# Scan items in pairs, a fixed order for one thread, and attention's products with V one pair of heads later, in a two-layer mixer and expert kernel

## The chip, the cores and the metric
The kernel runs on one core of a Trainium2 chip, as one launch. The metric is the device time of a run in microseconds; lower is better. The core's engines each work through their own queue in order: PE (matmul), DVE (vector), ACT (activation functions), POOL (GpSimd), and SP, which issues most of the DMAs.

## What is computed
Eight rows (batch entries) of 512 tokens with 256 channels pass through two layers. Layer 0: a conditioning block (gates, nine exponential moving averages over time, a layer norm), a Mamba block (a state space scan with 16 states for each of 512 inner channels), a linear map chosen by row, and a mixture of experts (top 2 of 8). Layer 1: a feed-forward block with LoRA experts, attention with 8 heads, an adapter with a layer norm, and a mixture of experts (top 4 of 32) beside a shared expert. The parts that the change touches:

```python
# Mamba, for every time step
dA = jnp.exp(dlt[:, None, :] * A[None])
h = dA * h + dlt[:, None, :] * B_t[:, :, None] * x_t[:, None, :]
y_t = jnp.einsum('bn,bnd->bd', C_t, h) + D * x_t
# attention of layer 1
attn = jax.nn.softmax(jnp.einsum('bnhr,bmhr->bhnm', Q, K), axis=-1)
out = jnp.einsum('bhnm,bmhd->bnd', attn, V)
# adapter of layer 1
return (y - mu) * jax.lax.rsqrt(var + EPS) * g + b
```

## The kernel before
Channels lie on partitions, the 512 time steps of a row on columns; nearly all data is float32. Two Python generators write the program, and a planner (the framework's list scheduler) places each instruction on its engine by its simulated time, with the order of writing as the priority. The order on each engine is then fixed, and the framework adds the semaphores.

**Thread x** (`thread_x`, L367) does the conditioning and Mamba blocks. `head_a` (L442) and `head_b` (L519) compute one row's inputs of the scan. Each head product goes through one of two PSUM buffers `gx`, and the ACT or DVE instruction that reads it is written right behind it. `split3` (L328) splits a float32 tile into three bfloat16 parts. The softplus part (L551 to L576) writes (delta, delta*x) tiles `dd` and stores them to DRAM as `pack`. From there `get_pack` (L591) reads them back, replicated over four groups of 32 partitions: 32 channels by 4 states fill the 128 partitions.

`scan(b)` (L612) has 64 items for a row: 4 channel blocks j, 4 state groups g, 4 quarters k. For item i, `begin` (L619) writes the decay `dA` = Exp on ACT (L623) and the input `h` = packed * B on POOL (L625); `run` (L645) has the recurrence on DVE (L651, one scan instruction over 512 columns, in place in `h`) and the product with C, which lies in PSUM (L652); `add` (L654) sums over states with four PE matmuls against `fold`, each into another 32 partitions of the same PSUM tile `yp` (L660). `begin` runs two items ahead; `dA` has 4 buffers and `h` has 8. After four groups, y is gated (L664, L665), and after 64 items the output projection and the store to `xa` follow (L684, L686). Two steps of the next row's head are written with every two items, and what is left of them before item 58.

**Thread y** (`thread_y`, L711) takes groups of rows (GROUPS: row 0; 1 and 2; 3 to 5; 6 and 7) through the rest of layer 0 and layer 1's feed-forward and attention, ending in `xb`. For each row, LoRA weights are merged first (L827 to L845), then come four pairs of heads (L862). For a pair: projections of Q and K (L870), four steps of `scores` (L883), `values` (L876) and `turn` (L901), and 32 matmuls of the products with V (L923). In `scores`, PE makes two score tiles (L889; 64 partitions each, at two places of the array), DVE takes the negative row maximum (L893), ACT takes Exp with the row sum (L896), and DVE takes the reciprocal (L897) and multiplies (L898). `turn` transposes on PE (L906). Tiles there have one buffer each unless a number says otherwise.

While thread y is written for group q, thread x is written for group q+1, in proportion (constants XROW and others at L36). With the last group the routers of the last mixture (`top4`, L930) are written; they use `layernorm` (L87: Sqrt on ACT at L99, reciprocal on DVE at L100). Last come the experts (`expert_tile`, L1060) and the final gather.

Of the kernel before, what the change touches and what calls it, by code (L numbers as in the profile page):

```python
# [35 lines left out]
XROW, YROW, YGROUP, YTILE, P4ROW = 269.0, 242.0, 20.0, 9.0, 10.0  # L36
# [15 lines left out]
def adaln_attn_ffn_kernel(ctx: ExitStack, tc: tile.TileContext, d: dict, out: bass.AP):  # L52
# [34 lines left out]
    def layernorm(pool, ps_tile, o, bufs=1):  # L87

        mean = ps_tile()
        mm(mean, [(onesdiv, o[:, k, :]) for k in range(KC)])  # L90
        cen = pool.tile([P, KC, T], F32, tag="ln_c", name="ln_c", bufs=bufs)
        nc.vector.tensor_tensor(cen, o, rep(mean, KC), ALU.subtract)
        yield 1
        sq = pool.tile([P, KC, T], F32, tag="ln_q", name="ln_q", bufs=bufs)
        nc.gpsimd.tensor_tensor(sq, cen, cen, ALU.mult)  # L95
        var = ps_tile()
        mm(var, [(onesdiv, sq[:, k, :]) for k in range(KC)])
        rstd = pool.tile([P, T], F32, tag="ln_r", name="ln_r", bufs=bufs)
        nc.scalar.activation(rstd, var, AF.Sqrt, bias=epst)  # L99
        nc.vector.reciprocal(rstd, rstd)  # L100
        return cen, rstd
# [53 lines left out]

    members = {}
# [12 lines left out]
    SYNC = mybir.DependencyInfo(mybir.DependencyClass.Sync, mybir.DependencyReason.DATA)  # L169

# [157 lines left out]
    def split3(pool, src, outs, p0, p1):  # L328
# [3 lines left out]
        nc.scalar.copy(outs[0], src)  # L332
        nc.vector.tensor_tensor(r, src, outs[0], ALU.subtract)
        nc.scalar.copy(m, r)
        nc.gpsimd.tensor_tensor(r, r, m, ALU.subtract)
        nc.scalar.copy(outs[1], m)
# [30 lines left out]
    def thread_x(wp, wk, ps):  # L367
# [74 lines left out]
        def head_a(b):  # L442

            x = rows[b]
            pt = gx()
            mm(pt[:64, :], [(Wn1[:, k, :], x[:, k, :]) for k in range(KC)])
            h1 = wk.tile([64, T], F32, tag="sg", name="h1", bufs=2)
            nc.scalar.activation(h1, pt[:64, :], AF.Gelu, bias=col("bn1", p=64))
            yield 3
            pt = gx()  # L450
            mm(pt[:8, :], [(Wn2, h1)])
            m8 = wk.tile([8, T], F32, tag="tr", name="m8", bufs=2)
            nc.scalar.activation(m8, pt[:8, :], AF.Sigmoid, bias=col("bn2c", p=8))
            split3(wk, m8, [m3[0:8, :], m3[32:40, :], m3[64:72, :]], 0, 8)
            yield 4
            ct = wk.tile([P, KC, T], F32, tag="ct", name="ct")
            for k in range(KC):
                nc.vector.tensor_tensor_scan(
                    ct[:, k, :], alpha[:, 0:1].to_broadcast([P, T]), x[:, k, :], 0.0, ALU.mult, ALU.add)
                yield 1.3  # L460
            gated = wk.tile([P, KC, T], F32, tag="gated", name="gated")
            for e in range(KC):
                pt = gx()
                mm(pt, [(Wg[:, k, ts(e, P)], x[:, k, :]) for k in range(KC)]
                   + [(Wg[:, KC + k, ts(e, P)], ct[:, k, :]) for k in range(KC)])
                sg = wk.tile([P, T], F32, tag="sg", name="sg", bufs=2)
                nc.scalar.activation(sg, pt, AF.Sigmoid, bias=col("bg", e))
                nc.gpsimd.tensor_tensor(gated[:, e, :], x[:, e, :], sg, ALU.mult)
            yield 4
            temporal = wk.tile([P, KC, T], F32, tag="ct", name="temporal")  # L470
            for i in range(8):
                pt = gx()
                mm(pt, [(three[0:72, i : i + 1].to_broadcast([72, P]), m3)])
                gm = wk.tile([P, KC, T], F32, tag="gm", name="gm")
                nc.vector.scalar_tensor_tensor(gm, rep(pt, KC), 0.5, gated, ALU.add, ALU.mult)
                yield 1.5
                for k in range(KC):
# [8 lines left out]
                    yield 2.2  # L486
            soma = wk.tile([P, KC, T], F32, tag="gm", name="soma")
            for e in range(KC):
                pt = gx()
                mm(pt, [(Wsoma[:, k, ts(e, P)], x[:, k, :]) for k in range(KC)])  # L490
                nc.scalar.activation(soma[:, e, :], pt, AF.Gelu, bias=col("bsoma", e))
            yield 3
            for e in range(KC):
                pt = gx()
                mm(pt, [(Wtemp[:, k, ts(e, P)], temporal[:, k, :]) for k in range(KC)])
                sg = wk.tile([P, T], F32, tag="sg", name="sg", bufs=2)
                nc.scalar.activation(sg, pt, AF.Sigmoid, bias=col("btemp", e))
                nc.gpsimd.tensor_tensor(soma[:, e, :], soma[:, e, :], sg, ALU.mult)
            yield 3
            cen = wk.tile([P, KC, T], F32, tag="cen", name="cen")  # L500
            sq = wk.tile([P, KC, T], F32, tag="gated", name="sq")
            for e in range(KC):
                pt = gx()
                mm(pt, [(Wout[:, k, ts(e, P)], soma[:, k, :]) for k in range(KC)])
                nc.scalar.copy(cen[:, e, :], pt)
                nc.scalar.activation(sq[:, e, :], pt, AF.Square)
                yield 2
            pt = gx()
            mm(pt, [(onesdiv, sq[:, k, :]) for k in range(KC)])
            rstd = wk.tile([P, T], F32, tag="sg", name="rstd", bufs=2)  # L510
            nc.scalar.activation(rstd, pt, AF.Ln, bias=epst)
            nc.scalar.activation(rstd, rstd, AF.Exp, scale=-0.5)
            nc.vector.tensor_tensor(cen, cen, rep(rstd, KC), ALU.mult)
            yield 3
            rows[b] = cen
            if b + 1 < NB:
                get_row(b + 1)

        def head_b(b):  # L519

            cn = rows[b]
            xc = wk.tile([P, 4, T], F32, tag="xc", name="xc")
            for j in range(4):
                pt = gx()
                mm(pt, [(W_in[:, k, ts(j, P)], cn[:, k, :]) for k in range(KC)])
                xp = xps[j % 2]
                nc.scalar.activation(xp[:, 3:], pt, AF.Identity, bias=wb[:, j : j + 1])
                cv = xc[:, j, :]
                nc.scalar.activation(cv, pt, AF.Identity, scale=col("convw", 4 * j + 3), bias=cb[:, j : j + 1])
                for i in range(3):  # L530
                    nc.vector.scalar_tensor_tensor(
                        cv, xp[:, i : i + T], col("convw", 4 * j + i), cv, ALU.mult, ALU.add)
                yield 3
            nc.scalar.activation(xc, xc, AF.Silu)
            nc.sync.dma_start(xzs[b % 2][:, :, 0, :], xc)
            for j in range(4):
                pt = gx()
                mm(pt, [(W_in[:, k, ts(4 + j, P)], cn[:, k, :]) for k in range(KC)])
# [3 lines left out]
            yield 5  # L542
            pt = gx()
            mm(pt[:96, :], [(W_x[:, j, :], xc[:, j, :]) for j in range(4)])
            dt = wk.tile([64, T], F32, tag="dt", name="dt")
            nc.scalar.copy(dt, pt[:64, :])
            bc3 = wk.tile([96, T], BF16, tag="bc3", name="bc3", bufs=2)
            split3(wk, pt[64:96, :], [bc3[64:96, :], bc3[32:64, :], bc3[0:32, :]], 64, 96)
            yield 3

            for j2 in range(2):  # L551
                dds, es = [], []
                for j in (2 * j2, 2 * j2 + 1):
                    pt = gx()
                    mm(pt, [(W_dt[:, ts(j, P)], dt)])

                    dd = wk.tile([P, 2, T], F32, tag=("gated", "ct")[j % 2], name="dd")
                    e = wk.tile([P, T], F32, tag="sg", name="sp_e", bufs=2)
                    nc.scalar.activation(e, pt, AF.Abs, bias=col("bdt", j))
                    nc.vector.tensor_scalar(dd[:, 0, :], pt, col("bdt", j), 0.0, ALU.add, ALU.max)  # L560
                    nc.scalar.activation(e, e, AF.Exp, scale=-1.0)
                    u = dd[:, 1, :]
                    nc.vector.tensor_scalar(u, e, 1.0, None, ALU.add)
                    nc.vector.scalar_tensor_tensor(e, u, 1.0, e, ALU.subtract, ALU.subtract)
                    dds.append(dd)
                    es.append(e)
                yield 3
                for dd in dds:
                    nc.scalar.activation(dd[:, 1, :], dd[:, 1, :], AF.Ln)
                for j, dd, e in zip((2 * j2, 2 * j2 + 1), dds, es):  # L570
                    u = dd[:, 1, :]
                    nc.gpsimd.tensor_tensor(u, u, e, ALU.subtract)
                    nc.gpsimd.tensor_tensor(dd[:, 0, :], dd[:, 0, :], u, ALU.add)
                    nc.gpsimd.tensor_tensor(dd[:, 1, :], dd[:, 0, :], xc[:, j, :], ALU.mult)
                    nc.sync.dma_start(packs[b % 2][j], dd)
                yield 3  # L576
            rows[b] = bc3

# [33 lines left out]
        def scan(b):  # L612

            bc3 = rows[b]
            items = [(j, g, k) for j in range(4) for g in range(4) for k in range(4)]
            yps, Cs, hs, dAs, xz = {}, {}, {}, {}, {}
            y8 = wk.tile([P, 4, T], F32, tag="y8", name="y8")

            def begin(i):  # L619
                j, g, k = items[i]  # L620
                t = got[b, j, k]
                dA = wk.tile([P, T], F32, tag="dA", name="dA", bufs=4)
# [14 lines left out]
                if j == 3 and b + 1 < NB and g == 3:  # L637
# [4 lines left out]
                    if k == 3:  # L642
                        get_B4(b + 1, 0)
# [558 lines left out]
```

## Time and profile before

| what | us |
|---|---|
| median of 3 runs (lowest, highest) | 4274.81 (4264.85, 4278.79) |
| the profiled execution, its own time | 4252.41 |
| span of the profile, first to last instruction | 4250.6 |
| DVE busy | 2670.9 |
| PE busy | 3440.5 |
| ACT busy | 1672.2 |
| POOL busy | 1565.8 |
| mean granted PE clock (share of full) | 0.889 |

The span has stages. To 150 us there is the head of row 0 alone. Its scan runs to 395 us, with nothing else but row 1's head. Three stages follow in which both threads run. From 2940 us on, thread y runs with the routers; from 3784 us the experts; from 4181 us the final gather. The profiled execution is 22.4 us below the median of the runs. In a line of the profile, L651 is a line of the kernel's source; "mean ns" is the mean length of one instruction; "idle before" is how long the engine had stood still, with what ended that wait.

### The profile page before, as it was taken

Reading aid. Unit: us, or ns where it says so; the run is one execution under the profiler, and the core shown is the slowest. Engines: PE = TensorE matmul, PEld = TensorE weight load, DVE = VectorE, ACT = ScalarE, POOL = GpSimd, SP = SyncE. Lnnn points to the kernel's source line nnn. Section 1 sums busy time; section 2 is a strip of 40 time slices with the busy share of each in tenths; the row PEclk is TensorE's granted clock in tenths of the full one; section 3 lists DMA queues with packets and bytes.
Section 4 is the critical chain, followed back from the end, with each engine's and each line's share of the span. In section 5 each row is a group of like instructions: output and inputs, shape, how many; then the busy total and the mean of one; then the engine's idle time right before and its main releaser. Section 6 shows DMA issues by size and latency. Waiting matters only on the chain. (4 is left out here: it accounts for less than half of the span.)

```text
span 4250.6 us, 36891 instructions
## 1 busy us (share of the span) xinstructions
PE 3440.5 (81%) x10964; PEld 1694.3 (40%) x10964; DVE 2670.9 (63%) x4290; ACT 1672.2 (39%) x2741; POOL 1565.8 (37%) x1222
## 2 busy tenths in 40 slices
PE   4556686887687888888758899889988999978994
PEld 2111352332254233333327443333456444436773
DVE  4698957886966686796892547575432454443336
ACT  2535463455366346445433443242223233322222
POOL 0456535434635333433542323231043111134552
PEclk7677798988798898999879999899989999989996
DMA  3235455324456423333346312213043312117776
GB/s 105 101 108 180 187 162 170 106 98 156 177 176 209 135 102 118 134 122 109 139 165 234 122 63 77 68 36 104 15 163 136 93 41 70 36 50 245 248 237 224
DMA packets 159372, 554.78 MB, mean 131 GB/s; under 512 B 27730, under 2 KB 34289, under 8 KB 146756
## 3 DMA queue, kind: packets, MB, share of 16 engines
q1 hardware_dynamic: 135076, 501.35, 35.2%
q0 software_dynamic: 24096, 51.08, 3.3%
q8 instruction: 87, 1.43, 0.1%
q14 instruction: 113, 0.93, 0.1%
HBM read 453.00 MB, written 234.82 MB: 162 GB/s over the span
## 5 line engine op out<-in xcount | busy, mean ns | idle before, releaser
L625 POOL TENSOR_TENSOR h<-packed,B 128x512 f32<-128x512 f32 x512 | 792.5, 1570 | 1054.2 <-PE yp L660 746.7
L651 DVE TENSOR_TENSOR_SCAN h<-dA,h 128x512 f32<-128x512 f32 x512 | 791.0, 1571 | 126.3 <-ACT dA L623 67.2
L623 ACT ACTIVATE dA<-packed,Aexp 128x512 f32<-128x512 f32 x512 | 359.8, 720 | 656.4 <-DVE h L651 446.5
L160 POOL DMA_INDIRECT tok<-ys,to_i x310 | 311.9, 1006 | 497.9 <-DVE ys L808 237.7
L660 PE MATMUL yp<-h,fold 128*32 128x512 f32 x1024 | 349.7, 704 | 156.9 <-DVE h L652 140.6
L923 PE MATMUL acc<-aT,V 128*128 128x512 f32 x1024 | 453.4, 597 | 5.3 <-ACT aT L907 3.2
L160 POOL DMA_INDIRECT tab<-row,si x192 | 197.4, 1028 | 465.5 <-issue 210.5
L652 DVE TENSOR_TENSOR h<-h,c 128x512 f32<-128x512 f32 x512 | 330.5, 672 | 29.0 <-PE c L78 28.2
L923 PEld LDWEIGHTS acc<-aT,V 128*128 128x128 f32 x1024 | 193.2, 191 | 245.9 <-issue 235.1
L78 PE MATMUL acc<-wv,c 128*128 128x512 f32 x512 | 270.2, 642 | 0.4
L78 PE MATMUL g<-qk 64*128 64x512 f32 x512 | 210.7, 681 | 54.9 <-ACT ex L896 28.6
L896 ACT ACTIVATE ex<-g,nm 128x512 f32<-128x512 f32 x256 | 173.8, 684 | 157.5 <-DVE nm L893 157.3
L78 PE MATMUL g<-xT,fw 128*128 128x256 f32 x960 | 233.6, 396 | 2.5 <-ACT h L801 1.9
L893 DVE TENSOR_REDUCE nm<-g 128x1 f32<-128x512 f32 x256 | 165.0, 681 | 100.8 <-PE g L78 100.8
L78 PE MATMUL acc<-fw,h 128*128 128x256 f32 x960 | 221.6, 383 | 3.5 <-DVE ys L808 1.8
L78 PEld LDWEIGHTS g<-xT,fw 128*128 128x128 f32 x960 | 188.0, 201 | 39.4 <-issue 6.8
L78 PEld LDWEIGHTS acc<-fw,h 128*128 128x128 f32 x960 | 182.7, 192 | 41.6 <-issue 12.4
L906 PE MATMUL acc<-ident,ex 128*128 128x128 f32 x1024 | 160.3, 286 | 47.9 <-DVE ex L898 16.2
L906 PEld LDWEIGHTS acc<-ident,ex 128*128 128x128 f32 x1024 | 122.6, 146 | 188.4 <-issue 69.3
L660 PEld LDWEIGHTS yp<-h,fold 128*32 128x32 f32 x1024 | 44.7, 115 | 364.1 <-DVE h L652 208.3
L479 DVE TENSOR_TENSOR_SCAN tr<-alpha,gm 128x512 f32<-128x512 f32 x128 | 181.4, 1435 | 5.0 <-POOL y L665 3.5
L78 PE MATMUL g<-xT,mw 128*128 128x256 f32 x760 | 183.1, 385 | 0.0
(280 smaller groups left out, 5458.3 us busy)
## 6 DMA issues: line engine op xcount, KB each, us to landing
fw<-in_fW SPq DMA_DIRECT2D x60, 1154.0 KB
tab<-zeros SPq DMA_DIRECT2D x32, 2112.0 KB
packed<-pack SPq DMA_DIRECT2D x128, 512.0 KB
mw<-in_mW SPq DMA_DIRECT2D x95, 384.0 KB
tab<-zeros SPq DMA_DIRECT2D x16, 2080.0 KB
xt<-tab SPq DMA_DIRECT2D x95, 264.0 KB
xz<-xzs SPq DMA_DIRECT2D x32, 512.0 KB
pack<-dd SPq DMA_DIRECT2D x32, 512.0 KB
```

The lines of the kernel that those rows point to most:

```text
L78: nc.tensor.matmul(o, lhsT, rhs, start=(i == 0), stop=(i == len(pairs) - 1))
L160: i = nc.gpsimd.indirect_dma_start(out=table_, out_offset=bass.IndirectOffsetOnAxis(ap=idx, axis=0), in_=src, in_offset=None, bounds_check ...
L479: nc.vector.tensor_tensor_scan(tr, alpha[:, 1 + i : 2 + i].to_broadcast([P, T]), gm[:, k, :], 0.0, ALU.mult, ALU.add)
L623: nc.scalar.activation(dA, t[:, 0, :], AF.Exp, scale=A[:, 4 * j + k, g : g + 1])
L625: nc.gpsimd.tensor_tensor(h, t[:, 1, :], B4s[b, g], ALU.mult)
L651: nc.vector.tensor_tensor_scan(h, dAs.pop(i), h, 0.0, ALU.mult, ALU.add)
L652: nc.vector.tensor_tensor(h, h, Cs[0], ALU.mult)
L660: nc.tensor.matmul(yps[j][32 * k : 32 * k + 32, :], fold, hs.pop(i + k), start=(g == 0), stop=(g == 3))
L893: nc.vector.tensor_reduce(nm, sp, AX.X, ALU.max, negate=True)
L896: nc.scalar.activation(ex, sp, AF.Exp, bias=nm, accum_out=den)
L906: nc.tensor.transpose(tp[:, m, :], ex[:, ts(m, P)], ident)
L923: nc.tensor.matmul(ys[k], V[:, m, C * u + P * k : C * u + P * (k + 1)], aTs[u][:, m, :], start=(u == 0 and m == 0), stop=(u == 1 and m == 3))
```

## The change
- **Scan in pairs.** Items 2m and 2m+1 share one `h` tile of 2 x 512 columns (4 buffers) and one of two lasting decay tiles. Column 0 of the second half of a decay tile is set to zero once, so the second recurrence starts anew, and one scan instruction covers 1024 columns; the product with C likewise. One loop runs over the items of all 8 rows. Work that follows an item (fold, gate, output projection) is put in a list `due` some items later.
- **Head in finer steps.** `head_a` and `head_b` become one generator `head`, which yields between a product and the instruction that reads it; one step goes with each item, and a second one in every twelve items. The scan of a row may start when the first two channel blocks' packs are on their way.
- **Fixed order.** `in_order` ties each instruction of thread x to the one before it on the same engine, without a semaphore, so the planner can't reorder thread x within an engine. `chain` ties matmuls that go to different parts of the array (fold, score pairs, LoRA pairs) one behind the other.
- **Attention.** The steps are written out over pairs of heads, with the products with V of the pair before between the first scores of a pair. The softmax's division goes to ACT. The LoRA weights use the buffers of `V`, `aT`, `wv` and `qk`.
- **Layer norm.** Sqrt and reciprocal become Ln and Exp on ACT.

The diff, cut to its core (the head is shown by one of its parts):

```diff
-XROW, YROW, YGROUP, YTILE, P4ROW = 269.0, 242.0, 20.0, 9.0, 10.0
+XROW, YROW, YGROUP, YTILE, P4ROW = 256.0, 242.0, 20.0, 9.0, 10.0
...
-        nc.scalar.activation(rstd, var, AF.Sqrt, bias=epst)
-        nc.vector.reciprocal(rstd, rstd)
+        nc.scalar.activation(rstd, var, AF.Ln, bias=epst)
+        nc.scalar.activation(rstd, rstd, AF.Exp, scale=-0.5)
...
+    def in_order(X):
+        last = {}
+        while True:
+            n = len(nc.cur_bb.bb.instructions)
+            c = next(X, None)
+            for i in nc.cur_bb.bb.instructions[n:]:
+                if i.engine in last:
+                    tc.add_manual_dep(i, last[i.engine].name, NOSYNC)
+                last[i.engine] = i
...
+            def taps(pt, j):
+                nc.scalar.activation(xps[j % 2][:, 3:], pt, AF.Identity, bias=wb[:, j : j + 1])
...
+            pj = [project(W_in, cen, 0)]
+            yield
+            for j in range(4):
+                if j > 0:
+                    conv(j - 1)
+                taps(pj[j], j)
+                pj.append(project(W_in, cen, j + 1))
+                yield
...
+        decays = []
+        for i in range(2):
+            t = wp.tile([P, 2, T], F32, tag=f"dA{i}", name=f"dA{i}")
+            nc.vector.memset(t[:, 1, 0:1], 0.0)
+            decays.append(t)
+        def begin(n):
+            b, j, g, k = items[n]
+            t = got[b, j, k]
+            u = n % 2
+            nc.scalar.activation(decays[n // 2 % 2][:, u, u:], t[:, 0, u:], AF.Exp, scale=A[:, 4 * j + k, g : g + 1])
+            if u == 0:
+                hs[n // 2] = wk.tile([P, 2, T], F32, tag="h", name="h", bufs=4)
+            nc.gpsimd.tensor_tensor(hs[n // 2][:, u, :], t[:, 1, :], B4s[b, g], ALU.mult)
...
+        def scan(m):
...
+            nc.vector.tensor_tensor_scan(h, dA, h, 0.0, ALU.mult, ALU.add)
+        def read(m):
+            b, j, g, k = items[2 * m]
+            nc.vector.tensor_tensor(hs[m], hs[m], rep(Cs[0], 2), ALU.mult)
+            if k == 2:
+                due.setdefault(2 * m + 2, []).append(lambda: add(2 * m - 2))
...
+            chain([nc.tensor.matmul(
+                yps[0][32 * k : 32 * k + 32, :], fold, hh[k // 2][:, k % 2, :], start=(g == 0), stop=(g == 3))
+                for k in range(4)])
...
+        for n in range(N):
...
+            if n % 2 == 0:
+                scan(n // 2)
+            else:
+                read(n // 2)
+            if n + 2 < N:
+                begin(n + 2)
+            for f in due.pop(n, ()):
+                f()
+            next(H, None)
+            if i % 12 == 4:
+                next(H, None)
+            yield 4
...
+                    ms = [nc.tensor.matmul(
+                        sps[u], qk[64 * u : 64 * u + 64, 0, ts(i, P)], qk[64 * u : 64 * u + 64, 1, :],
+                        start=True, stop=True) for u in (1, 0)]
+                    chain(ms)
+                    for e in read:
+                        tc.add_manual_dep(ms[0].ins, e.name, SYNC)
...
+                def norm(hp, i):
+                    den = dens.pop((hp, i))
+                    nc.vector.reciprocal(den, den)
+                    for u in range(2):
+                        ex = exs[hp, i, u]
+                        nc.scalar.activation(ex, ex, AF.Identity, scale=den[:, u : u + 1])
...
+                for hp in range(HP + 1):
+                    if hp < HP:
+                        scores(hp, 0)
+                        yield 1
+                    if hp > 0:
+                        yield from out(hp - 1, 0)
+                    if hp < HP:
+                        norm(hp, 0)
+                        scores(hp, 1)
+                        yield 1
+                    if hp > 0:
+                        add(0)
+                        yield from out(hp - 1, 1)
+                    if hp < HP:
+                        norm(hp, 1)
+                        if hp + 1 < HP:
+                            weights(hp + 1)
+                        for m in range(4):
+                            values(hp, m)
...
-        X = filling(thread_x(
+        X = filling(in_order(thread_x(
```

## The prediction
> **What bounds the kernel now.** I read the page's totals first, then a table of busy time by stage, then the costly groups, the shortest and median scan, two PE timelines, and the waits of DVE and ACT.
>
> ```profile
> span 4250.6 us, 36891 instructions
> ...
> PE 3440.5 (81%) x10964; PEld 1694.3 (40%) x10964; DVE 2670.9 (63%) x4290; ACT 1672.2 (39%) x2741; POOL 1565.8 (37%) x1222
> ```
> ```profile
> core 0: us, PE busy (x) PEld busy (x) DVE busy (x) ACT busy (x) POOL busy (x), PEclk, DMA share, GB/s
> 0.00:150.00 150.00, 73.14 (x145) 28.41 (x145) 68.88 (x103) 54.34 (x70) 22.36 (x30) 0.77 0.37 107
> 150.00:395.00 245.00, 148.32 (x254) 33.20 (x254) 225.48 (x199) 113.73 (x146) 147.12 (x89) 0.70 0.35 126
> 395.00:1067.00 672.00, 515.90 (x1510) 226.07 (x1509) 509.48 (x641) 319.43 (x484) 300.79 (x209) 0.85 0.43 148
> 1067.00:2085.00 1018.00, 831.85 (x2471) 367.26 (x2472) 775.31 (x1019) 504.72 (x776) 439.62 (x306) 0.89 0.41 142
> 2085.00:2940.00 855.00, 726.25 (x2356) 356.20 (x2354) 525.57 (x812) 320.90 (x565) 285.54 (x214) 0.92 0.31 108
> 2940.00:3784.00 844.00, 794.63 (x2589) 412.15 (x2589) 361.81 (x878) 245.88 (x475) 169.78 (x168) 0.97 0.24 81
> ```
> The totals name no bound; the stages do. In **solo** (150 to 395, row 0's scan) DVE is busy 92%. In **A** (395 to 1067, two rows of thread x beside one of y) and **B** (to 2085, three beside two) PE is at 77% and 82%, DVE at 76% in both: neither is full, they take turns. **C** (to 2940, two rows beside up to three) leans to PE, 85% against 61%. **D** (to 3784, y and the routers) is PE's, 94%. What follows isn't touched.
>
> ```profile
> L651 DVE TENSOR_TENSOR_SCAN h<-dA,h 128x512 f32<-128x512 f32 x512 | 791.0, 1571 | 126.3 <-ACT dA L623 67.2 <-POOL h L625 59.0
> L660 PE MATMUL yp<-h,fold 128*32 128x512 f32 x1024 | 349.7, 704 | 156.9 <-DVE h L652 140.6 <-DVE y L664 15.8
> L652 DVE TENSOR_TENSOR h<-h,c 128x512 f32<-128x512 f32 x512 | 330.5, 672 | 29.0 <-PE c L78 28.2
> L898 DVE TENSOR_SCALAR ex<-ex,den 128x512 f32<-128x512 f32 x256 | 161.8, 634 | 3.3
> ```
> ```profile
> L267 DVE TENSOR_TENSOR_SCAN sc_e<-one,sc_t x5: 160/165/224, 469.5 to 3803.8; 128x8 f32<-128x8 f32 x4, 128x32 f32<-128x32 f32 x1
> ...
> L651 DVE TENSOR_TENSOR_SCAN h<-dA,h x512: 1181/1212/9429, 150.3 to 2901.9; 128x512 f32<-128x512 f32 x171
> ```
> ```profile
> 200.41 2.51 PE L660 MATMUL yp<-h,fold 128*32 128x512 f32 x4 [4.43 <-DVE h L652]
> ...
> 1526.20 1.05 PE L660 MATMUL yp<-h,fold 128*32 128x512 f32 x4
> ```
> ```profile
> DVE dd L560 <- DMA pack<-dd: 25.6, 4, 13.3
> ...
> DVE xc L531 <- ACT xc L529: 12.1, 5, 5.3
> ...
> ACT cen L505 <- PE gx L78: 30.2, 9, 5.7
> ```
> The fences show: the scan's fixed price (8 columns cost 0.160 us, 512 cost 1.181 at best, 1.545 in the mean); a fold group of four matmuls that takes 2.51 us strung out and 1.05 together; and engines of thread x waiting on the step just before.
>
> **The change part by part.** The sum stands against the profiled execution's 4252.4 us; the median shown is 22.4 above it, and I add 22 at the end.
>
> *Scan in pairs.* One column costs (1181-160)/504 = 2.03 ns, so 1024 columns cost 2.22 us against 2 x 1.181: 0.14 saved. The product with C at 1024 columns is nearest to L92's 128x1024 product, mean 1.213, against 2 x 0.672: 0.13 saved. A pair saves 0.27 us. The 0.364 us that a scan now takes above its best stands beside POOL's products (clean near 1.26, mean 1.57); I keep it per column. If a long scan waits once where two waited twice, a pair gains 0.36 more; if it waits as for three, it loses 0.36: 32 pairs x 0.36 = 12 us of DVE a row either way, 94 in eight.
>
> The Trainium skill (SBUF — State Buffer, "Who interferes with whom") speaks against it: a DVE instruction with two SBUF inputs holds the port pair shared with GpSimd to its end, so POOL would wait out a scan of twice the length. The trace agrees with a lock, since scans cluster at 1.2 and 2.2 us. By that rule a blocked POOL product takes up to 1.26 + 2.22 = 3.5 us.
>
> Were all 64 products of a row that slow (1.26 + 2.22), POOL would need 223 us a row beside its 35 of others, over solo's 245; at today's mean it needs 64 x 1.57 = 100. I take the latter.
>
> *Softmax's division.* L898 leaves DVE (0.63 each), and 256 reciprocals (39.1 us) become 128. ACT gains 256 instructions at the 0.684 of L896, 175 us; its busy share is 48%, 50%, 38% and 29% in A to D, which hides it. Uncovered it would be 22 us per y row.
>
> *Per stage, if DVE sets the pace* (its work cut, its share kept): A: 66 pairs x 0.27 + 23.4 (L898 there) + 2.4 = 44, over 0.76 = 58 us. B: 95 x 0.27 + 46.3 + 4.8 = 77, over 0.76 = 101. C: 63 x 0.27 + 41.6 + 4.9 = 64, over 0.61 = 104.
>
> *If PE sets it.* The chain holds a fold group together: 349.7/256 = 1.37 becomes 1.05, 0.32 each. A 65 groups = 21, over 0.77 = 27; B 96 = 31, over 0.82 = 38; C 63 = 20, over 0.85 = 24. Score and lora pairs are chained too; the trace doesn't separate their overlap well, between 0 and (210.7/256 - 0.68) = 0.14 us a score pair. I take that only in D.
>
> I take the middle of both for A (42) and B (70), since the shares are equal, and PE's 24 for C. **134**.
>
> *Head in finer steps, fixed order.* Each engine now meets a product one step after it was made. DVE rows that should go: in B dd 25.6 and 11.7, xc 12.1, s_r 9.7, y 7.4, gm 6.7, cen 6.2, xr 4.3 = 84; in A the same names come to 82. Much of that idle time is where PE is next anyway: between 0 and 166, I take a quarter, 41. In solo DVE works 32 x 0.27 = 9 less and the pack waits there (5.3 and 4.1) may go: 15. At the start, pack 0 is fetched before the other delta work (its store was issued at 133, its loads at 138.7): 5.
>
> *Costs.* More steps with another ACT function between decays: I count 14 such groups a row, so up to 28 table loads; the rows of thread x hold some 190 loads in 8 rows, 24 each. 4 x 7 x 1.283 = 36 us, between 0 and 36: 18. Weight tiles of y now share attention's buffers, so they arrive only after the last products with V; the gather of the next row covers that, and one load's 2 to 4 us a row if not.
>
> *New waits.* A step's first score matmul waits for both Exps of the step before. Both score banks had to be read before the second anyway, so at most one Exp (0.684) a step is added, 128 steps, 88 us; behind it on PE stand x's folds and the next products. A product with V or a projection lies before it in every step, so I take 0. A row's closing products now come some six items into the next row: in solo 6 x 245/64 = 23 us after its last scan, where 11 passed (scan's end 395.2, store 406.4). Thread y starts up to 12 us later, with thread x running on meanwhile: 0.
>
> *Products with V a pair later.* No work is added; 16 matmuls now cover the wait from scores to exponentials. In D PE is idle 49 us in all, which bounds it. 48 score pairs x 0.14 = 7, bubbles 3, and the last layernorm's 3.35 us reciprocal becomes an Exp of 0.63: 3. Together 13. DMAs are the same in number; POOL's and SP's queues carry the same issues, x's in written order.
>
> Sum: 134 + 41 + 15 + 5 + 13 - 18 = 190. 4252.4 - 190 + 22 = **4085 us**.
>
> **The rivals.** *PE paces A to C alone:* 27 + 38 + 24 + 15 + 5 + 13 = 122, so 4152. For it: PE's share is the higher one in all three. Against: its digits hold waits for DVE (L660 156.9).
>
> *The pairs don't save:* long scans pay the lock's 94 us; at half weight over 0.76 that is 62 back, 4147.
>
> *Fixed order stalls (slower):* a decay Exp can no longer pass an ACT instruction of the head that waits for PE. From 395 to 2940 such rows are cen 30.2, B 33.4, xp 17.9, m 16.1, s_m 15.6, dd 23.5 = 137 us, harmless now. Behind them would stand the Exp, the next scan (only one pair ahead, 3.1 + 1.2 us) and fold. With all 36 of table loads (18 more than I took) and 160 score maxima each meeting half a scan more (1.1 us, 176) that is 331 lost: 4085 + 331 = 4416. It decides once these stalls pass 190 us. For it: DVE's wait for dA (67.2) is small only as long as ACT runs ahead. Against: the step delay exists to have PE's result ready.
>
> **How the numbers follow.** Main 0.46, its own range 3960 to 4150; PE alone 0.15; no saving 0.06; stalls 0.29, from 4290 to 4500; near no change 0.04. Within 0.3% is what a measurement here can't tell from none. Faster: 0.46 + 0.15 + 0.06, less 0.02 whose upper ends touch the band: 0.65. Same 0.06. Slower 0.29. The range runs from 3960, main's end, to 4370, taking in the lower third of the stall case and leaving out about 0.2.
>
> **What would show it.** Scans: 256 with a mean near 2.95 us. A fold group near 1.05. L898's work on ACT. DVE's rows dd, xc, s_r, cen gone. Stages A, B near 610 and 930 us. It is wrong if DVE's wait for dA grows past 200 us, if POOL's product passes 2.5 us, or if PE's idle time before scores grows in D.

## The result and the profile after

| | before | after | ratio, 95% interval |
|---|---|---|---|
| median, 20 runs each, us | 4274.97 | 4268.49 | 0.9987 [0.9976, 0.9998] |
| profiled execution, us | 4252.4 | 4274.6 | |
| its span, us | 4250.6 | 4272.7 | |

The change is worth 0.13%, within the 0.3% that the prediction counts as no change, where 190 us were forecast. The profiled execution of after is an ordinary one (6 us above its median), that of before lies 23 below its own; so stage lengths are compared to some 0.5% only.

The page's totals and traffic, after:

```profile
span 4272.7 us, 35960 instructions
...
PE 3266.5 (76%) x10964; PEld 1657.9 (39%) x10964; DVE 2497.8 (58%) x3485; ACT 1835.4 (43%) x2950; POOL 1675.3 (39%) x1222
...
DMA  4555666445354312211235312213044112117776
GB/s 104 206 183 206 223 244 212 143 176 197 125 176 157 90 64 68 86 64 62 87 130 205 112 47 67 69 37 105 13 181 146 51 50 75 33 51 247 241 241 219
```

DVE is busy 173 us less than before and PE 174 us less. The work did leave both engines, and the span did not follow. The second thing to see is the traffic: the first seven slices carry up to 244 GB/s and the middle is near 64. The same rows of before:

```profile
DMA  3235455324456423333346312213043312117776
GB/s 105 101 108 180 187 162 170 106 98 156 177 176 209 135 102 118 134 122 109 139 165 234 122 63 77 68 36 104 15 163 136 93 41 70 36 50 245 248 237 224
```

Busy time by stage, after, cut where thread x's last scan of a row ends (rows 0, 2, 5, 7) and where y stores its last row (columns: PE, PEld, DVE, ACT, POOL, granted clock, DMA share, GB/s):

```profile
161.00:419.00 258.00, 106.33 (x247) 28.46 (x247) 209.41 (x140) 115.38 (x149) 158.49 (x91) 0.62 0.53 189
419.00:1060.00 641.00, 469.66 (x1505) 217.18 (x1506) 490.77 (x477) 353.45 (x516) 318.91 (x208) 0.85 0.56 199
1060.00:2057.00 997.00, 773.82 (x2492) 355.81 (x2490) 762.71 (x799) 543.88 (x818) 495.77 (x312) 0.87 0.31 102
2057.00:2911.00 854.00, 675.54 (x2261) 339.38 (x2261) 470.12 (x593) 341.56 (x594) 314.36 (x213) 0.88 0.29 93
2911.00:3766.00 855.00, 796.28 (x2621) 407.01 (x2619) 288.18 (x703) 313.07 (x576) 154.06 (x152) 0.97 0.24 79
```

Cut the same way, in us:

| | head | solo | A | B | C | D | tail |
|---|---|---|---|---|---|---|---|
| before | 150 | 245 | 652 | 1017 | 839 | 858 | 489 |
| after | 161 | 257 | 642 | 996 | 855 | 855 | 506 |
| fills mended (e2) | 150 | 245 | 616 | 1004 | 847 | 844 | 497 |
| fills and finish mended (e10) | 151 | 245 | 595 | 995 | 845 | 842 | 505 |

A and B gained 10 and 21 us where 42 and 70 (and part of 41) were forecast; head, solo and C lost 11, 12 and 16. The tail's code is the same in all four but for one layer norm: its 489 to 506 is the noise of this table.

The costly groups of after:

```profile
L762 POOL TENSOR_TENSOR h<-packed,B 128x512 f32<-128x512 f32 x512 | 836.5, 1657 | 994.5 <-PE yp L801 592.0
L787 DVE TENSOR_TENSOR_SCAN h<-dA,h 128x1024 f32<-128x1024 f32 x256 | 720.4, 2814 | 192.1 <-POOL h L762 140.1
...
L791 DVE TENSOR_TENSOR h<-h,c 128x1024 f32<-128x1024 f32 x256 | 310.7, 1214 | 26.3 <-PE c L78 21.9
...
L78 PE MATMUL c<-bc,quads 96*128 96x512 bf16 x128 | 58.7, 458 | 242.6 <-DVE h L791 242.5
...
L801 PE MATMUL yp<-h,fold 128*32 128x512 f32 x1024 | 210.1, 727 | 1.8 <-DVE h L791 1.8
```

The long scan's mean is 2.81 us and the fold's busy time fell from 349.7 to 210.1. But PE's wait moved: its idle time before the fold went from 156.9 to 1.8, and before the product that spreads C, which the fixed order puts ahead of the fold, from 48.1 (the line of before below) to 242.6. Together these waits grew by 39.

```profile
L78 PE MATMUL c<-bc,quads 96*128 96x512 bf16 x128 | 55.3, 432 | 48.1 <-DVE h L652 45.9 <-ACT bc L337 1.9
```

Where the traffic came from shows in the rows of the zero fills (`filling` issues them on SP's queue, 2.1 MB each, to clear the tables `tab` and `tok`), first of before, then of after; the columns are count, shortest/median/longest issue in ns, first and last start:

```profile
L153 SPq DMA_DIRECT2D tab<-zeros x48: 494/555/5400, 28.0 to 1934.7; - x48
L153 SPq DMA_DIRECT2D tok<-zeros x8: 526/530/547, 1998.7 to 2258.9; - x8
```
```profile
L153 SPq DMA_DIRECT2D tab<-zeros x48: 491/538/2536, 21.1 to 939.2; - x48
L153 SPq DMA_DIRECT2D tok<-zeros x8: 476/496/1142, 963.9 to 1103.0; - x8
```

The 56 fills end at 1103 us instead of 2259. `filling` issues one in every four steps of thread x; a step was two scan items and is now one, so the same rule issues twice as many a row. It is a line that the diff doesn't touch, fed by a loop that it does.

### The profile page after: what moved, and what is told of

Same layout as the page of the kernel before. It is cut to its first block, busy times and chain, and to the rows that moved or that the text cites. A ratio compares the mean times of both kernels' runs of the same rounds, so it can differ in the third digit from the quotient of the medians.

```text
span 4272.7 us, 35960 instructions
## 1 busy us (share of the span) xinstructions
PE 3266.5 (76%) x10964; PEld 1657.9 (39%) x10964; DVE 2497.8 (58%) x3485; ACT 1835.4 (43%) x2950; POOL 1675.3 (39%) x1222
## 5 line engine op out<-in xcount | busy, mean ns | idle before, releaser
L762 POOL TENSOR_TENSOR h<-packed,B 128x512 f32<-128x512 f32 x512 | 836.5, 1657 | 994.5 <-PE yp L801 592.0
L787 DVE TENSOR_TENSOR_SCAN h<-dA,h 128x1024 f32<-128x1024 f32 x256 | 720.4, 2814 | 192.1 <-POOL h L762 140.1
L759 ACT ACTIVATE dA<-packed,Aexp 128x512 f32<-128x512 f32 (+1 forms) x512 | 351.4, 715 | 493.6 <-DVE h L787 342.9
L174 POOL DMA_INDIRECT tok<-ys,to_i x310 | 329.2, 1062 | 440.6 <-DVE ys L974 196.5
L1099 PE MATMUL acc<-aT,V 128*128 128x512 f32 x1024 | 463.7, 601 | 4.9 <-issue 3.7
L791 DVE TENSOR_TENSOR h<-h,c 128x1024 f32<-128x1024 f32 x256 | 310.7, 1214 | 26.3 <-PE c L78 21.9
L78 PE MATMUL c<-bc,quads 96*128 96x512 bf16 x128 | 58.7, 458 | 242.6 <-DVE h L791 242.5
L801 PE MATMUL yp<-h,fold 128*32 128x512 f32 x1024 | 210.1, 727 | 1.8 <-DVE h L791 1.8
L1061 PE MATMUL g<-qk 64*128 64x512 f32 x512 | 177.9, 666 | 33.8 <-ACT ex L1074 22.4
L1083 ACT ACTIVATE ex<-ex,den 128x512 f32<-128x512 f32 x256 | 170.8, 715 | 31.3 <-DVE den L1080 31.0
```

What stands on the lines that cost most here:

```text
L78: nc.tensor.matmul(o, lhsT, rhs, start=(i == 0), stop=(i == len(pairs) - 1))
L174: i = nc.gpsimd.indirect_dma_start(out=table_, out_offset=bass.IndirectOffsetOnAxis(ap=idx, axis=0), in_=src, in_offset=None, bounds_check ...
L759: nc.scalar.activation(decays[n // 2 % 2][:, u, u:], t[:, 0, u:], AF.Exp, scale=A[:, 4 * j + k, g : g + 1])
L762: nc.gpsimd.tensor_tensor(hs[n // 2][:, u, :], t[:, 1, :], B4s[b, g], ALU.mult)
L787: nc.vector.tensor_tensor_scan(h, dA, h, 0.0, ALU.mult, ALU.add)
L791: nc.vector.tensor_tensor(hs[m], hs[m], rep(Cs[0], 2), ALU.mult)
```

## The experiments

Each ratio is to the kernel before on the same chip, with its 95% interval; there 0.1% is 4.25 us. Unless another base is named, the edit is to after, whose own ratio is 0.9987. Every edit also lets the planner place all instructions anew, so a ratio holds the named edit together with whatever order came out.

**Four at once: which part loses?** e1 drops `in_order`; e2 gives the fills their old density; e3 is the kernel before with after's attention; e4 is after with the attention of before.

The edit of e1, and of e2:

```diff
-        X = filling(in_order(thread_x(
+        X = filling(thread_x(
```
```diff
-            if fills and n % 4 == 1 and (n > 44 or n < 4 * first):
+            if fills and n % 8 == 1 and (n > 58 or n < 4 * first):
```

Of e4, by its core (e3 puts after's lines into before):

```diff
-                lora = wk.tile([64, C + 1024], F32, tag="V", name="lora")
+                lora = wk.tile([64, C + 1024], F32, tag="lora", name="lora")
...
-                    chain(ms)
+                        mm(pt[:, ts(k, 256)], [(lora[0:32, ts(k, P)], lora[0:32, C + 256 * w : C + 256 * (w + 1)])])
...
-                wqks, wvs, qks, Vs, aTs, exs = {}, {}, {}, {}, {}, {}
```

> The changed kernel without the tie of thread x to its written order on each engine; nothing else differs. Theory W (the fixed order puts new waits at the head of the queues: PE waited 242 us for the product with C before its C matmul, against 46 before): the planner may pass those, so 40 to 100 us faster than the changed kernel (4170 to 4230) and PE's wait for L791 under 100 us. Theory F (the zero fills of the tables, which go out one per four steps of thread x, now go out twice as densely and delay the scan's loads): within 10 us of 4268. Theory L (rows are finished later, so thread y starts later): within 15 us.

> The changed kernel with a zero fill at every eighth step of thread x, from step 58, so that a row gets about 8 fills as in the kernel before, not 16. Theory F: the head ends near 150 us instead of 161 and row 0's scan takes some 245 instead of 258 us, 20 to 40 us faster in all (4230 to 4250). Theories W and L: within 10 us of 4268.

> The kernel before with the change's thread y alone (score and LoRA pairs chained, division on ACT, products with V one pair later, shared buffers); thread x as before. From the times between a group's first xa and last xb in the two profiles (654 to 613, 1002 to 930, 1007 to 1002, 823 to 803 us) the attention part is worth 20 to 60 us where thread x lets it: 4215 to 4255. If all of the change's work is off the path, within 10 us of 4275.

> The changed kernel with thread y as before: thread x's pairs, fine steps and fixed order, and the layer norm by Ln and Exp. Theories W, F and L (thread x's part loses what attention gains): 4285 to 4320, slower than the kernel before by 10 to 45 us. If both parts are off the path, within 10 us of 4275.

Measured: e1 1.0361 [1.0341, 1.0381], e2 0.9920 [0.9901, 0.9938], e3 1.0154 [1.0131, 1.0176], e4 1.0038 [1.0024, 1.0052].

e1: the fixed order helps the new program by 3.7%; it is not what ate the gain. e2: the fills cost 0.7%, some 28 us, and head and solo return to 150 and 245. In these two stages PE, DVE, ACT and POOL run the same instructions in the same order in both traces, so the 23 us gained there are the fills' alone. What they delay shows in the waits for the loads of the packs (columns: total, times, longest us), after and then e2:

```profile
POOL h L762 <- DMA packed<-pack: 203.8, 49, 14.7
...
ACT dA L759 <- DMA packed<-pack: 127.7, 31, 16.3
```
```profile
POOL h L762 <- DMA packed<-pack: 112.6, 30, 12.1
ACT dA L759 <- DMA packed<-pack: 93.3, 23, 13.6
```

e3 was a miss: the new attention costs 1.5% beside the old thread x, and by e4 is worth 0.5% beside the new one. So the parts don't add, and which other part turns the sign wasn't tried.

**Prices of single terms.** e5 closes the rows that thread y waits for (0, 2, 5, 7) right behind their last fold. e6 does scan and C product one item at a time again. e7 halves the fold's weights and issues every fold matmul twice into the same sum, 1024 matmuls more. e8 puts the division back on DVE. e9 does the products with V at the end of their own pair.

e5:

```diff
-                due.setdefault(n + 5, []).append(lambda: gate(b, j, n + 6))
+                if j == 3 and b in (0, 2, 5, 7):
+                    close(b)
+                else:
+                    due.setdefault(n + 5, []).append(lambda: gate(b, j, n + 6))
...
+        def close(b):
...
+            for e in range(KC):
+                pt = gx()
+                mm(pt, [(W_out[:, j, ts(e, P)], y8s[b][:, j, :]) for j in range(4)])
+                nc.vector.tensor_tensor(x[:, e, :], x[:, e, :], pt, ALU.add)
+            nc.sync.dma_start(xa[b], x)
+            done.add(b)
```

e6:

```diff
-            nc.vector.tensor_tensor_scan(h, dA, h, 0.0, ALU.mult, ALU.add)
+            for u in range(2):
+                nc.vector.tensor_tensor_scan(
+                    h[:, T * u : T * (u + 1)], dA[:, T * u : T * (u + 1)], h[:, T * u : T * (u + 1)], 0.0, ALU.mult, ALU.add)
...
-            nc.vector.tensor_tensor(hs[m], hs[m], rep(Cs[0], 2), ALU.mult)
+            for u in range(2):
+                nc.vector.tensor_tensor(hs[m][:, u, :], hs[m][:, u, :], Cs[0], ALU.mult)
```

e7:

```diff
+        nc.vector.tensor_scalar(fold, fold, 0.5, None, ALU.mult)
...
-                yps[0][32 * k : 32 * k + 32, :], fold, hh[k // 2][:, k % 2, :], start=(g == 0), stop=(g == 3))
-                for k in range(4)])
+                yps[0][32 * k : 32 * k + 32, :], fold, hh[k // 2][:, k % 2, :], start=(g == 0 and v == 0),
+                stop=(g == 3 and v == 1)) for v in range(2) for k in range(4)])
```

e8:

```diff
-                        nc.scalar.activation(ex, ex, AF.Identity, scale=den[:, u : u + 1])
+                        nc.vector.tensor_scalar(ex, ex, den[:, u : u + 1], None, ALU.mult)
```

e9, by its core:

```diff
-                for hp in range(HP + 1):
+                for hp in range(HP):
...
-                    if hp > 0:
-                        yield from out(hp - 1, 0)
...
-                            if m == 0 and hp > 0:
-                                add(1)
```

> The changed kernel, but the last row of each group (0, 2, 5, 7) is gated, projected and stored right behind its last fold, not in steps over six items. Theory L (thread y waits at the handovers for the late store: 44 and 59 us idle in the changed kernel, 7 and 16 before): xa 10 to 20 us behind the last scan instead of 30 to 52, 40 to 80 us faster than the changed kernel (ratio to before 0.980 to 0.990). Rival (both threads are paced together, so an earlier start is given back): ratio 0.996 to 1.001.

> The changed kernel with each scan of 1024 columns split back into two of 512, and each product with C into two, at the same places of the order; tiles and buffers as in the change. DVE gets about 256 x 0.27 = 70 us more work. If DVE's work sets the pace of solo, A and B: 60 to 100 us slower than the changed kernel (ratio to before 1.013 to 1.022). If the saved work is off the path (theory N): ratio 0.995 to 1.003.

> The changed kernel with the fold halved and each fold matmul made twice into the same sum: the same result, with 1024 more PE records, some 145 us of PE work, at the same place; about what chaining the folds saved (349.7 to 210.1 us busy). If PE's work sets the pace of A to C: 80 to 140 us slower than the changed kernel (ratio 1.017 to 1.032). Theory N: 0 to 20 us slower (0.999 to 1.004).

> The changed kernel with the softmax's division back on DVE (256 instructions of about 0.63 us), the reciprocal still one per two heads. If DVE's work sets the pace of A and B: 60 to 110 us slower than the changed kernel (ratio 1.013 to 1.025). Theory N: ratio 0.995 to 1.003. If the division on ACT held up the transposes, it is faster: below 0.994.

> The changed kernel with attention's products with V at the end of their own pair of heads; all else of the change kept. If moving them a pair later is what makes the new attention pay beside the fixed order (attention alone cost 1.5% in the old thread x and gained 0.5% in the new one): 30 to 80 us slower than the changed kernel (ratio to before 1.006 to 1.018). If PE has enough other work there (theory N): ratio 0.995 to 1.002.

| | ratio | against after |
|---|---|---|
| e5 early finish | 0.9939 [0.9923, 0.9955] | late finish costs 0.5%, 20 us |
| e6 single scans | 1.0025 [1.0013, 1.0037] | pairs are worth 0.4%, 16 us |
| e7 double folds | 1.0127 [1.0108, 1.0145] | costs 1.4%, 60 us |
| e8 division on DVE | 1.0014 [0.9999, 1.0030] | division on ACT is worth 0.3%, 12 us |
| e9 own pair | 1.0000 [0.9985, 1.0014] | 0.1%, intervals touch: not measurable |

e6 puts 100 us of work back on DVE (2597.6 busy against 2497.8) for 16 us, and e8 101 us (2599.2) for 12. So DVE's work counts 0.12 to 0.16 us a us. e8's is a net price: it takes 134 us off ACT, and with the 162 us of division on DVE the planner moved copies of `aT` to ACT (104 left on DVE, 145 in after). For PE, the fold line of e7 (before the bar: busy, mean ns):

```profile
L802 PE MATMUL yp<-h,fold 128*32 128x512 f32 x2048 | 348.6, 710 | 0.0
```

138.5 us more fold for 60 us: 0.43 us a us (0.54 by PE's busy time in all, which rose by 110), at least 2.7 times DVE's price and little over half. e5 gains 0.5%. Before, a row's output was stored 11, 20, 21 and 35 us after the last scan of rows 0, 2, 5 and 7; after, 30, 45, 39 and 52; in e5, 16, 27, 14 and 53. Row 7 didn't improve. From its last store until rows 2 and 5 are stored, y still waits 43 and 55 us in e5, 44 and 59 in after (7 and 16 before). So the early finish pays, but that it pays by a shorter wait of y is not shown.

**Do the two losses add, and is it the density?** e10 is e2 and e5 together. e11 is the kernel before with fills twice as dense. e12 and e13 are e10 with one edit each: POOL's three products of a softplus in steps of their own (and the head's extra step twice as often), and 290 instead of 256 for `XROW`, the planner's cost of a row.

e11 (against before):

```diff
-            if fills and n % 4 == 1 and (n > 44 or n < 4 * first):
+            if fills and n % 2 == 1 and (n > 36 or n < 2 * first):
```

e12 and e13 (against e10):

```diff
+                yield
...
-            soft4(0)
+            yield from soft4(0)
...
-            if i % 12 == 4:
+            if i % 6 == 4:
```
```diff
-XROW, YROW, YGROUP, YTILE, P4ROW = 256.0, 242.0, 20.0, 9.0, 10.0
+XROW, YROW, YGROUP, YTILE, P4ROW = 290.0, 242.0, 20.0, 9.0, 10.0
```

> The changed kernel with both menders: fills at every eighth step (0.992 alone) and the early finish of a group's last row (0.994 alone). If the two losses add up: ratio 0.985 to 0.990 (F and L are two causes). If they are one delay seen twice: 0.991 to 0.994.

> The kernel before with its zero fills twice as dense (every second step of thread x instead of every fourth), so 16 a row as in the changed kernel; nothing else. Theory F: 15 to 40 us slower than before (1.0035 to 1.0095), in the head, solo and A. If the fills hurt only the changed order: 0.998 to 1.002.

> As e10_fills_finish, with the three POOL instructions that end each softplus (fixed order puts all three before the next scan inputs; DVE waited 8.9 us at once there in row 0) in steps of their own, and two extra head steps in twelve items. If POOL's fixed order costs about 5 us a row at two places: 20 to 60 us faster than e10 (ratio 0.974 to 0.985). Rival (the wait moves elsewhere): within 0.003 of e10.

> As e10_fills_finish with the constant XROW at 290, not 256: thread x is written ahead, so that its rows end when thread y has done 88% of its group. If thread x's lag at the handovers costs (33 and 55 us of idle thread y in e10): 30 to 70 us faster than e10 (ratio to before 0.966 to 0.975). Rival (thread y's engines are slowed as much as thread x gains): 0.979 to 0.985.

Measured: e10 0.9820 [0.9802, 0.9838], e11 1.0220 [1.0202, 1.0238], e12 0.9929 [0.9912, 0.9946], e13 0.9846 [0.9826, 0.9866].

e10 beats both kernels, by 1.8% and 1.7%. Singly the two mends brought 0.7% and 0.5%, together 1.7%: neither makes the other needless. In e11 one line in the old program costs 2.2%, more than expected, with the same shift of traffic to the first slices and more waiting for packs on ACT (180.7 us against 132.2 before; POOL's is unchanged, 190.6 and 190.2):

```profile
GB/s 103 188 174 227 212 219 192 186 156 165 155 164 136 99 54 78 88 41 52 85 97 182 129 115 46 81 58 57 63 110 166 106 42 65 40 40 229 246 243 225
```
```profile
ACT dA L623 <- DMA packed<-pack: 180.7, 47, 9.2
```

But the fills are not all of these 2.2%. Against before, A is 48 us longer and B 41, and e11's last fill starts at 1128 us, 31 us into B, which then carries less traffic than before (92 GB/s against 143). The planner also placed the instructions otherwise: ACT's order differs from the 43rd instruction on, DVE's from the 105th. How much of e11 is the fills' and how much the order's is not shown. Row of B in e11 (columns as in the table by stage):

```profile
1096.80:2154.60 1057.80, 844.46 (x2466) 372.77 (x2464) 779.83 (x1018) 496.67 (x772) 430.72 (x305) 0.88 0.28 92
```

e12 and e13 are misses: e12 is 1.1% slower than e10, and e13 brings no gain (its interval overlaps e10's), as its rival expected. e13 did what it was meant to do: rows 2 and 5 are stored 17 and 31 us before y ends its group, so y has nothing to wait for. B fell from 995 to 943 us and C grew from 845 to 896. So taking y's wait at the handovers away brought nothing. e12 was aimed at these lines, POOL's timeline in the solo stage of e2 (start, us):

```profile
370.66 1.27 POOL L667 TENSOR_TENSOR dd<-dd 128x512 f32<-128x512 f32 x1
372.01 1.27 POOL L668 TENSOR_TENSOR dd<-dd,xc 128x512 f32<-128x512 f32 x1
373.25 1.26 POOL L762 TENSOR_TENSOR h<-packed,B 128x512 f32<-128x512 f32 x1
374.48 1.25 POOL L666 TENSOR_TENSOR dd<-dd,sp_e 128x512 f32<-128x512 f32 x1
375.81 1.26 POOL L667 TENSOR_TENSOR dd<-dd 128x512 f32<-128x512 f32 x1
377.15 1.26 POOL L668 TENSOR_TENSOR dd<-dd,xc 128x512 f32<-128x512 f32 x1
```

Three products of the head stand between the two halves of one scan's input, and the scan waits 8.9 us for the second half. The wait is there, but the kernel with the three spread out is slower.

**With the losses mended, does DVE's work count?** e14 and e15 are e10 with the edits of e6 and e8. e16 is e10 with the fills sparser still:

```diff
-            if fills and n % 8 == 1 and (n > 58 or n < 4 * first):
+            if fills and n % 9 == 1 and (n > 64 or n < 9 * first):
```

> As e10_fills_finish with scans and products with C split back into 512 columns (70 us more DVE work). If the two losses hid the pairs' worth: 60 to 100 us slower than e10 (0.996 to 1.006). If DVE's work doesn't pace the stages: 5 to 25 us slower (0.983 to 0.988).

> As e10_fills_finish with the division back on DVE (some 162 us more DVE work, as much less on ACT). If the two losses hid its worth: 60 to 110 us slower than e10 (0.996 to 1.008). If DVE's work doesn't pace the stages: within 20 us of e10 (0.978 to 0.987).

> As e10_fills_finish with a fill at every ninth step from step 64 (about as sparse as the number of steps allows). If the fills still cost in proportion to their density: 5 to 15 us faster than e10 (0.978 to 0.981). If what they delay is hidden at this density: within 0.002 of e10 (0.980 to 0.984).

Measured: e14 0.9846 [0.9824, 0.9869], e15 0.9859 [0.9837, 0.9881], e16 0.9843 [0.9823, 0.9864]. Pairs are worth 0.3% (11 us) and the division 0.4% (17 us), about what they were before the mending, though the intervals touch e10's. So a mended program isn't one that DVE paces either. No gain from still sparser fills can be told (e16).

## Why the prediction was wrong

**Where it failed.** "DMAs are the same in number; POOL's and SP's queues carry the same issues" holds for the count and fails for the times: the fills went twice as dense, 0.7% (e2). "Thread y starts up to 12 us later, with thread x running on meanwhile: 0" fails too: rows 0, 2 and 5 are stored 19, 25 and 18 us later behind their last scan than before, and closing them early is worth 0.5% (e5), though by which wait isn't shown. Together 1.7%, 71 us (e10 against after).

**DVE's pace.** The middle of "DVE paces" and "PE paces" was taken because their busy shares are equal. In A and B that put half of 58 and 101, some 80 us, on DVE's work (with C's 24 the terms make 136, not 134). The runs show 16 and 12 us (11 and 17 mended), 28 together, over all stages. The pairs did get cheaper as computed: e6's 100 us are 0.39 a pair where 0.27 was worked out. What failed first is the step from a busy share to the pace. The work, too, was counted too high. In A and B DVE was to lose 44 and 77 us; cut as in the table, it went from 497 and 774 us (the rows of before below) to 491 and 763. The prediction takes the division off DVE and leaves all else in place, but `aT`, `V` and `qk` are copied by whichever engine the planner picks, and with the division on ACT more of these copies went to DVE, those of `aT` above all (first before, then after):

```profile
395.00:1047.00 652.00, 504.56 (x1485) 222.35 (x1485) 497.05 (x626) 314.40 (x476) 294.48 (x205) 0.86 0.43 146
1047.00:2064.00 1017.00, 833.19 (x2480) 368.51 (x2478) 773.75 (x1018) 505.94 (x777) 437.86 (x305) 0.89 0.42 143
```
```profile
L907 DVE COPY aT<-acc 128x512 f32<-128x512 f32 x52 | 35.0, 677 | 11.6 <-PE acc L906 11.2
```
```profile
L1093 DVE COPY aT<-acc 128x512 f32<-128x512 f32 x145 | 98.4, 686 | 122.7 <-PE acc L1092 107.4 <-remote 10.2 <-issue 4.9
```

In solo, where DVE was busy 92% and the case looked clearest, after's work with the fills mended (e2) takes DVE 209.60 us instead of 225.48 in the same 245:

```profile
150.00:395.00 245.00, 103.14 (x247) 27.04 (x247) 209.60 (x140) 115.41 (x148) 158.12 (x91) 0.63 0.37 128
```

The 16 us saved came back as idle time on DVE, 11 of it in waits for POOL's products (22.3 us, not counting the 23.8 before the first scan, against 11.2), so "solo: 15" was 0. "Start: 5" was 0 as well (head 150 in both).

**PE's part.** The sign was right, the size of the fold mis-taken: a group is eight records, not four, so there are 128 groups, and each fell from 2.73 us (349.7/128) to 1.64 (210.1/128). That is 140 us off PE where some 80 were counted. At e7's 0.43 it would be 60 us, an estimate; against it stand 39 us more of waiting at the C product. A group that isn't interrupted takes 1.06 us (65 of 128 in after), as foreseen, but only at full clock. PE's clock is granted at 1.0 or 0.5 at any one time; in row 0's scan, where the mean is 0.62, 11 of 16 groups of eight records with nothing between them take 1.94. So the 2.51 us that the prediction read in solo as four matmuls strung out, against 1.05 in B, were two matmuls, and most of the difference was the clock.

**Products with V later.** Bubbles of 3 us were priced for it in D; e9 measured 0.1% with touching intervals, so no effect that can be told from none. The other 10 us of that term weren't tried alone.

**The rivals.** "Fixed order stalls" falls with e1, which frees the order and is slower; and in after DVE waits less for dA, 46.7 us against 67.2. "PE paces A to C alone" would have been a gain of 122 us; at e7's price, which stays near half, PE's work isn't the whole pace either. "The pairs don't save" is nearly right in its outcome, not its reason. The Trainium skill (SBUF — State Buffer, "SBUF: two separate sides") says that a DVE instruction with two SBUF inputs and a GpSimd one that reads SBUF lock each other out: the first to start has the shared ports for its whole length. From this, up to 1.26 + 2.22 = 3.5 us for a POOL product was estimated. Here are the product and the scan of after, shortest/median/longest ns:

```profile
L762 POOL TENSOR_TENSOR h<-packed,B x512: 1250/1273/3461, 154.7 to 2904.6; 128x512 f32<-128x512 f32 x171
L787 DVE TENSOR_TENSOR_SCAN h<-dA,h x256: 2253/2292/9452, 161.2 to 2909.0; 128x1024 f32<-128x1024 f32 x128
```

The longest is 3.46 us. Over 2.5 us are 75 of 512 products, against 4 before and none in e14, which is e10 with short scans. The trace agrees with the rule in the worst case; the mean rose only from 1.57 to 1.66, so the long scans can still gain a little. "Near no change" had 0.04 and came out, for a reason that none of the cases held: the gain (1.8% once mended) and two losses (1.7%) are of one size.

**Signs foretold.** Scans 256 with a mean of 2.81 (2.95) and division on ACT: right. DVE's waits in B for dd, xc, s_r and cen were to be gone: they fell, from 37.3, 12.1, 9.7 and 6.2 us to 7.1, 2.2, 5.1 and 5.5, and the wait of PE before the C product grew instead. The signs of being wrong hardly showed: DVE's wait for dA fell, POOL's product passed 2.5 us in 75 cases but not in the mean, and PE's idle time before scores in D stayed at 0.4 us. Stages A and B 641 and 997 (610, 930): wrong, and with both losses mended 595 and 995, so A came through with the mends and B did not.

**Still open.** e10 gains 1.8%, some 75 us, of 190 forecast. DVE's mis-sized term (80 to 28) and the two zeros (20) account for 72 of the missing 115. What is left can lie in terms that no run tries alone: the quarter of X's waits (41); the table loads on ACT, of which the traces hold 328 after and 286 before, 1.28 us each; and C, which was to gain 24 us and lost 16 (6 in e10) although PE has 24 us and DVE 60 us less work there. PE's clock is a rival that the prediction and the runs leave out: the granted clock in C fell from 0.91 to 0.88 (0.87 in e10), its mean from 0.889 to 0.868 (0.873). It doesn't order the runs by itself, since e7 has 0.879 and is slower than after, but what it cost is open. Not left is y's wait at the handovers, which e13 removes without a gain. Why the new attention loses beside the old thread x is not known.

## What to carry to other kernels

When a loop's steps are cut finer, look for everything that counts steps: here a background transfer that the diff doesn't touch went twice as dense. Where a second thread starts on a row's end, look at when the row's last store goes out, and price that too. Where the framework may choose an engine, work taken off one engine can come back as other work: compare its busy time after the change. An engine's busy share is not its price: put some work back on it and measure, before a saving of busy time is entered in a sum.

## What the runs showed of the hardware

Background transfers delayed small loads on the critical path. With the same instructions in the same order on PE, DVE, ACT and POOL, the head took 161 us and row 0's scan 257 with the denser fills (147 and 189 GB/s), and 150 and 245 with the sparser ones (86 and 128 GB/s; after and e2).
